# Four convolution and attention layers on eight images: the last two images' tail in a written order, and a normalised image transposed in its own tile

## The chip, the cores and the metric

The kernel runs on one core of a Trainium2 chip. A core has five engines with queues of their own: TensorE (PE, matrix products and transposes), VectorE (DVE), ScalarE (ACT), GpSimd (POOL) and SyncE (SP, which issues most transfers). Each works through its queue in order and waits for the others through semaphores. The metric is the device time of the whole program in microseconds (us). The profile is of one execution, with its own time, and shows every instruction on its engine.

## The reference

Eight images of 384 channels and 32 x 32 positions, all in fp32, go through four layers, each with a residual:

```python
x = x + L0(gn(x))   # attention over 8 heads, q, k, v by depthwise 3x3 + 1x1
x = x + L1(gn(x))   # four experts of two 384x384 layers, mixed by a router
x = x + L2(gn(x))   # quantised depthwise 3x3, then quantised 1x1
x = x + L3(gn(x))   # deformable attention
```

`gn` normalises over groups of channels; here there are 32 groups for 384 channels. In layer 3, q is a 1x1 product. A depthwise 5x5 convolution of stride 2 on q, with a batch norm and Gelu, gives for each of three groups of 128 channels and each of 256 places two offsets and a modulation. The normalised image is sampled bilinearly at the moved places (outside the image counts as zero), multiplied by the sigmoid of the modulation, and gives k and v. Six heads of 64 channels attend from 1024 queries to 256 keys; a 1x1 product with bias ends the layer.

## The kernel before

An image lies in SBUF as 128 partitions x 3 chunks (of 128 channels) x 1024 positions. `HALF` is 512 positions, which is one PSUM bank. `big` gives one of two PSUM tiles of two banks, `fbank` one of three single banks, `vbank` the one that is left. In SBUF, the pool `im` has five image-sized buffers that are used in turn, and there are tiles with fixed names (`hd0` to `hd3`, `h1`, `om0` to `om2`), which `third` and `pl.one` hand out.

Layer 0 runs over all images first, then routing. From there the kernel goes image by image: `layers(b)` is a generator that issues layers 2 and 3 of image b in steps and says with each `yield` about how long it leaves PE without work. `layer1(pl, b + 1)` is a list of units (matmuls of the expert layers: `ph`, L1491, and `y`, L1512) of the next image. The loop adds up the times and issues a unit whenever 2.6 us (`UNIT`) are due, so that the matmuls of the next image fill the gaps of this one. What comes out is a fixed order of instructions in each engine's queue; nothing is decided at run time.

Within `layers(b)`: the depthwise taps of layer 2 on DVE (L1634), the products `pw` (L1647), group norm (statistics on DVE; `gna` and `gnb`, L117 and L128, two tiny matmuls that sum over partitions; the reciprocal square root as a power on POOL, L98), the normalised image `h3`, q (`pq`, L1684), the transposes `px` of `h3` into positions x channels (L1707), written by ACT and DVE in turn into another image tile, `xT`; 25 taps of the offset convolution `off` on DVE (L1754), Gelu; `pom`, three products that spread offsets and modulation over all partitions (L1780, L1781), Tanh and positions on ACT and DVE; then for eight blocks of 128 image positions a bilinear weight `wt` (Abs and Relu on ACT, L1815 and L1818, product of x and y weights on POOL, L1819) and three matmuls that sum `xT` with it (`xsb`, `xs`, L1823); k and v (L1837, L1846). The attention has six units (three pairs of heads x two halves of the queries): scores `s` (L1862), exponentials `p` on ACT (L1879), the sum of the two key blocks' exponentials `p01` on POOL (L1924), `pav` (L1888), `pss` (L1901, the denominators), and on DVE the transposed copy `tu` (L1936) and the division. `pf` (L1991) is the last product, and DVE adds it to the image (L1999), which goes out.

For image 6 the loop stops at the step after Gelu (the `yield None`), issues the rest of image 7's layer 1, and then the tail begins: one step of image 7's layers for each step that image 6 has left, after that image 7 alone. Image 7 differs in a few ways: its layer-2 taps run during its layer 1, each as an output chunk is done (`convolve`); group norm of layer 2 is worked in afterwards (`layer2_last`: constants for the borders are added on DVE, then ACT normalises, L1605); its PSUM tiles are single banks (`pair`), and its h3 and xT lie in halves in the `hd` tiles.

Of the kernel before, what the change touches and what calls it, by code (L numbers as in the profile page):

```python
# [7 lines left out]
F32 = mybir.dt.float32  # L8
# [5 lines left out]
N = H * W  # L14
# [41 lines left out]
def tile_kernel(ctx: ExitStack, tc: tile.TileContext, i: dict, out: bass.AP):  # L56
# [1345 lines left out]
    def pair(last, name):  # L1402


        if last:
            return None, [fbank(f"{name}_{h}") for h in range(2)]
        t = big(name)
        return t, [t[:, :HALF], t[:, HALF:]]

# [154 lines left out]
    def convolve(pl, xt, c, h):  # L1564
# [7 lines left out]
        lo, hi = ((0, H // 2 - 1), (H // 2 - 1, H))[h]  # L1572
        nc.vector.tensor_scalar(
# [11 lines left out]
    def layer2_last(b, xt):  # L1585

        y = ahead["y"]
        ga, dm = gn_spread(gn_mean(ahead["st"], f"d2_{b}"), f"d2_{b}", fbank)
        edge = wd.tile([P, KC, 8], F32, name="edge_last")
        nc.vector.tensor_scalar(edge, edge2, ga[:, 0:1], None, ALU.mult)  # L1590
        for c in range(KC):
            dst = y[:, c, :].rearrange("p (h w) -> p h w", h=H)
            for d, e, axis in (
                (dst[:, 0 :: H - 1, :], edge[:, c, 0:2], 2), (dst[:, :, 0 :: W - 1], edge[:, c, 2:4], 1)
            ):
                nc.vector.tensor_tensor(d, d, e.unsqueeze(axis).to_broadcast(list(d.shape)), ALU.add)
            d = dst[:, 0 :: H - 1, 0 :: W - 1]
            nc.vector.tensor_tensor(
                d, d, edge[:, c, 4:8].rearrange("p (a b) -> p a b", a=2), ALU.add
            )  # L1600
        ss = gn_scale(ga, dm, f"d2_{b}", fbank)
        sums = wd.tile([P, KC], F32, name="sums_last")
        nc.vector.tensor_scalar(sums, sum2, ss[:, 1:2], None, ALU.mult)
        for c in range(KC):
            nc.scalar.activation(  # L1605
                y[:, c, :], y[:, c, :], AF.Identity, bias=sums[:, c : c + 1], scale=ss[:, 0:1]
            )
        yield 5.0
        yield from pointwise(b, xt, [y[:, c, :] for c in range(KC)])
# [29 lines left out]
    def pointwise(b, xt, y):  # L1639

        last = b == B - 1
        for m in range(KC):
            whole, pw = pair(last, f"pw{b}_{m}")
            for h in range(2):
                hs = slice(h * HALF, (h + 1) * HALF)
                for c in range(KC):
                    nc.tensor.matmul(  # L1647
                        pw[h], lhsT=upw2[:, c, m * P : (m + 1) * P], rhs=y[c][:, hs],
                        start=(c == 0), stop=(c == KC - 1),
                    )  # L1650
            xm = xt[:, m, :]
            outs = zip((xm[:, :HALF], xm[:, HALF:]), pw) if last else [(xm, whole)]
            for d, f in outs:
                nc.vector.scalar_tensor_tensor(d, f, mp, d, ALU.mult, ALU.add)
            nc.sync.dma_start(out=x2_dram[b, :, m, :], in_=xm)
            yield 0.0

    def layer3(pl, b, xt, put, general):

        last = b == B - 1  # L1660
# [4 lines left out]
        ss = gn_finish(st, f"d3_{b}", fbank if last else vbank)  # L1665
        yield 5.0

        if last:
            h3 = [third(pl, h, f"h3_{b}_{h}") for h in range(2)]
            for h in range(2):  # L1670
                for c in range(KC):
                    affine(h3[h][:, c, :], xt[:, c, h * HALF : (h + 1) * HALF], ss)
        else:
            t = pl.img(f"h3_{b}")
            for c in range(KC):
                affine(t[:, c, :], xt[:, c, :], ss)
            h3 = [t[:, :, :HALF], t[:, :, HALF:]]
        yield 3.0
        q = pl.img(f"q_{b}")
        for m in range(KC):  # L1680
            whole, pq = pair(last, f"pq3_{b}_{m}")
            for h in range(2):
                for c in range(KC):
                    nc.tensor.matmul(  # L1684
                        pq[h], lhsT=wq3[:, c, m * P : (m + 1) * P], rhs=h3[h][:, c, :],
                        start=(c == 0), stop=(c == KC - 1),
                    )
            if last:
                for h in range(2):
                    evac(q[:, m, h * HALF : (h + 1) * HALF], pq[h])  # L1690
            else:
                evac(q[:, m, :], whole)
            yield 0.0

        T2 = NT8 // 2
        if last:
            xT = [third(pl, 2 + h, f"xT_{b}_{h}").rearrange("p a n -> p (a n)") for h in range(2)]
        else:
            t = pl.img(f"xT_{b}").rearrange("p c n -> p (c n)")
            xT = [t[:, : T2 * C], t[:, T2 * C :]]  # L1700
        xT = [t.rearrange("p (t c) -> p t c", t=T2) for t in xT]
        for t in range(0, NT8, 2):
            h, t2 = divmod(t, T2)
            whole, px = pair(last, f"px_{b}_{t}")
            for k in range(2):
                for c in range(KC):
                    nc.tensor.transpose(  # L1707
                        px[k][:, c * P : (c + 1) * P],
                        h3[h][:, c, (t2 + k) * P : (t2 + k + 1) * P], ident,
                    )  # L1710
            if last:
                for k in range(2):
                    evac(
                        xT[h][:, t2 + k, :].rearrange("p (q c) -> p c q", c=KC),
                        px[k][:, :C].rearrange("p (c q) -> p c q", c=KC),
                    )
            else:
                evac(
                    xT[h][:, t2 : t2 + 2, :].rearrange("p t (q c) -> p t c q", c=KC),
                    whole.rearrange("p (t n) -> p t n", t=2)[:, :, :C].rearrange(  # L1720
                        "p t (c q) -> p t c q", c=KC
                    ),
                )
            yield 0.4

        if last:
            off = pl.one([P, KC, HALF], "h1", f"off_{b}").rearrange("p c n -> p (c n)")
            off = off[:, : NG * LS].rearrange("p (g h w) -> p g h w", g=NG, h=HS)
        else:
            off = pl.flat([P, NG, HS, HS], f"off_{b}")  # L1730
        src = q.rearrange("p g (h w) -> p g h w", h=H)

        def span(s):
            lo = max(0, (-s + 1) // 2)
            hi = min(HS - 1, (H - 1 - s) // 2)
            return lo, hi

        for t in (12, *range(12), *range(13, 25)):
            dy, dx = t // 5 - 2, t % 5 - 2
            (r0, r1), (c0, c1) = span(dy), span(dx)  # L1740

            gs = [None] if r1 - r0 + 1 == HS else range(NG)
            for g in gs:
                if g is None:
                    d = off.rearrange("p g h w -> p (g h) w")[:, :, c0 : c1 + 1]
                    f = q.rearrange("p g (h w) -> p (g h) w", h=H)[:, dy : : 2, :]
                else:
                    d = off[:, g, r0 : r1 + 1, c0 : c1 + 1]
                    f = src[:, g, 2 * r0 + dy : 2 * r1 + dy + 1 : 2, :]
                f = f[:, :, 2 * c0 + dx : 2 * c1 + dx + 1 : 2]  # L1750
# [484 lines left out]
```

## Time and profile before

| | us |
|---|---|
| median of three runs | 3484.91 (3483.53 to 3489.36) |
| profiled execution, its own time | 3480.29 |
| its span, first to last instruction | 3478.5 |
| PE busy in it | 3372.7 (97%) |
| DVE, ACT, POOL busy | 1708.2, 1298.5, 200.1 |
| last `y` of image 7's layer 1 ends | about 3266 |
| last `pf` ends | about 3471 |
| mean granted PE clock | 0.989 of full |

A group's busy time is the union of its instructions; "idle before" is the time its engine stood still ahead of it, and the releaser is the instruction whose semaphore came last. In fp32 each matmul leaves two records: one of 512 columns takes 0.86 us in a row of its kind and has two records of some 0.6 us that overlap. [...] Transfers play no part in what follows: the 16 DMA engines are busy for 18% of the time at most in any stretch of the tail.

### The profile page before, as it was taken

The page shows a single profiled execution, that of the slowest core. Times are in us where ns is not written, and L with a number is a line of the kernel's source. Part 1 is how long each engine was busy: PE and PEld are TensorE (multiplying, and loading weights), DVE is VectorE, ACT ScalarE, POOL GpSimd, SP SyncE. Part 2 cuts the span into 40 slices and gives each one's busy share as a digit, 9 for nine tenths or more (in the row PEclk, how much of TensorE's full clock was granted, in tenths as well). Part 3 has the DMA queues.
Part 4 walks back from the last instruction along what each step waited for, and adds up shares of the span by engine and source line. Part 5 has one row for each costly group of instructions (what it writes and reads, how often), then busy time and mean ns, then how long its engine had stood idle before and what let it go on. Part 6 is the DMA issues. An engine that isn't in the chain of part 4 may idle for free.

```text
span 3478.5 us, 44959 instructions
## 1 busy us (share of the span) xinstructions
PE 3372.7 (97%) x18599; PEld 1449.4 (42%) x18599; DVE 1708.2 (49%) x2926; ACT 1298.5 (37%) x1514; POOL 200.1 (6%) x231
## 2 busy tenths in 40 slices
PE   6999999999999999998999999999999999999888
PEld 2333434343434343443344445344453444434344
DVE  8942232323232323234266375663755637557763
ACT  5655444444444444433222322323223232331232
POOL 2100000000000000000000200102001010010022
PEclk9999999999999999999999999999999999999999
DMA  9972121212121212023600111101111011110000
GB/s 355 299 208 79 27 79 27 79 27 79 27 80 26 80 27 79 27 79 102 247 24 19 47 46 35 40 18 36 57 35 40 18 35 58 35 39 19 18 1 37
DMA packets 86260, 234.01 MB, mean 67 GB/s; under 512 B 21673, under 2 KB 21897, under 8 KB 79131
## 3 DMA queue, kind: packets, MB, share of 16 engines
q1 hardware_dynamic: 83882, 222.75, 19.8%
q10 hardware_dynamic: 1248, 4.72, 0.4%
q8 instruction: 150, 2.46, 0.3%
q0 software_dynamic: 912, 3.53, 0.3%
q14 instruction: 68, 0.55, 0.0%
HBM read 145.77 MB, written 75.59 MB: 64 GB/s over the span
## 4 chain that ended last, share of the span: by engine, by line
PE 43%; DVE 8%; DMA 1%; ACT 1%; POOL 0%; issue 0%; DVEq 0%; POOLq 0%; ACTq 0%; SPq 0%
PE y L1512 12%; PE ph L1491 10%; DVE y L1634 4%; PE pq L1684 4%; PE pw L1647 3%; PE pf L1991 3%; PE s L1862 2%; PE pav L1888 2%; DVE off L1754 1%; PE xsb L1823 1%; DVE hd L1477 1%; PE pss L1901 1%; PE pk L1837 1%; PE pv L1846 1%; PE plog L1231 1%; DMA o<-o 1%
## 5 line engine op out<-in xcount | busy, mean ns | idle before, releaser
L827 ACT ACTIVATE p<-s 128x1024 f32<-128x1024 f32 x512 | 496.3, 1021 | 365.7 <-PE s L820 365.5
L835 PE MATMUL pav<-p,vt 64*64 64x512 f32 x4096 | 494.5, 588 | 0.0
L1512 PE MATMUL y<-hd,w_sb 128*128 128x512 f32 x1080 | 487.1, 599 | 3.5 <-DVE hd L1477 3.5
L1491 PE MATMUL ph<-h,w_sb 128*128 128x512 f32 x1104 | 487.0, 595 | 1.9 <-ACT h L1440 1.8
L820 PE MATMUL s<-qk,qk 48*64 48x512 f32 x2944 | 355.0, 592 | 0.0
L1491 PEld LDWEIGHTS ph<-h,w_sb 128*128 128x128 f32 x1104 | 206.8, 190 | 262.3 <-issue 248.6
L1512 PEld LDWEIGHTS y<-hd,w_sb 128*128 128x128 f32 x1080 | 199.7, 191 | 249.0 <-issue 235.4
L835 PEld LDWEIGHTS pav<-p,vt 64*64 64x64 f32 x4096 | 167.4, 133 | 274.6 <-issue 274.4
L796 DVE COPY ta<-pav 128x512 f32<-128x512 f32 (+1 forms) x65 | 44.3, 682 | 475.3 <-PE pav L835 475.3
L1501 ACT ACTIVATE hd<-ph,b_sb 128x512 f32<-128x512 f32 x180 | 122.8, 682 | 309.9 <-PE ph L1491 309.9
L574 PE MATMUL pk<-xs,cws_sb 32*32 32x496 f32 (+3 forms) x3840 | 181.9, 605 | 38.8 <-POOL xs L402 29.4
L1754 DVE SCALAR_TENSOR_TENSOR off<-q,dw_sb,off 128x225 f32<-128x225 f32 (+3 forms) x432 | 215.8, 556 | 1.8
L1634 DVE SCALAR_TENSOR_TENSOR y<-h,tap,y 128x961 f32<-128x961 f32 (+1 forms) x168 | 203.0, 1229 | 0.5
L820 PEld LDWEIGHTS s<-qk,qk 48*64 48x64 f32 x2944 | 108.6, 133 | 212.0 <-issue 191.1
L1879 ACT ACTIVATE p<-s 128x1024 f32<-128x1024 f32 x96 | 96.2, 1023 | 165.7 <-PE s L1862 134.2
L81 DVE COPY qk<-pq 128x512 f32<-128x512 f32 x46 | 31.8, 692 | 251.8 <-PE pq L258 251.8
L1477 DVE TENSOR_TENSOR hd<-hd,cb 128x512 f32<-128x512 f32 x180 | 122.4, 685 | 37.7 <-ACT hd L1501 37.5
L574 PEld LDWEIGHTS pk<-xs,cws_sb 32*32 32x32 f32 (+1 forms) x3840 | 77.2, 111 | 141.9 <-issue 57.8
L1924 POOL TENSOR_TENSOR p<-p,p 128x1024 f32<-128x1024 f32 x48 | 113.4, 2364 | 330.0 <-ACT p L1879 329.9
L820 PE MATMUL s<-ql,ql 48*64 48x512 f32 x1024 | 128.2, 592 | 0.2 <-ACT p L827 0.2
L1991 PE MATMUL pf<-att,wp_sb 128*128 128x512 f32 x288 | 127.4, 597 | 0.0
L711 PE MATMUL pv<-wv_sb,g 128*128 128x384 f32 x384 | 127.1, 489 | 0.0
(341 smaller groups left out, 3734.5 us busy)
## 6 DMA issues: line engine op xcount, KB each, us to landing
rqk<-y SPq DMA_DIRECT2D x96, 256.0 KB
g<-rqk SPq DMA_DIRECT2D x96, 256.0 KB
xs<-in_xs_dram SPq DMA_DIRECT2D x56, 384.0 KB
g<-rv SPq DMA_DIRECT2D x48, 256.0 KB
xh<-in_x_dram SPq DMA_DIRECT2D x48, 256.0 KB
f<-in_x_dram SPq DMA_DIRECT2D x24, 512.0 KB
f<-o SPq DMA_DIRECT2D x24, 512.0 KB
o<-ot SPq DMA_DIRECT2D x42, 256.0 KB
```

Of the source, the lines that this page charges most:

```text
L574: nc.tensor.matmul(banks[r][cols[q]].rearrange("p (h w) -> p h w", w=W)[:, :, c0:c1], lhsT=cws[rs, c, 2 * h + g, x, w], rhs=src[rs, :, c0 ...
L711: nc.tensor.matmul(pv[:, :C], lhsT=acts[b][2][:, c, t * P : (t + 1) * P], rhs=w_in[2][:, c, :], start=(c == 0), stop=(c == KC - 1),)
L820: nc.tensor.matmul(s[64 * k : 64 * k + 64, j * HALF : (j + 1) * HALF], lhsT=kt[r, k0 : k0 + 64], rhs=qt[r, h * HALF : (h + 1) * HALF], sta ...
L827: nc.scalar.activation(p, s, AF.Exp, scale=scale)
L835: nc.tensor.matmul(pav[k][64 * j : 64 * j + 64, :], lhsT=vts[b % 2][r, kc, 2 * hd : 2 * hd + 2, :].rearrange("p a b -> p (a b)"), rhs=p[r, ...
L1477: nc.vector.tensor_tensor(hd, hd, state["cb"], ALU.mult)
L1491: nc.tensor.matmul(ph, lhsT=w1[:, e, c, dc * P : (dc + 1) * P], rhs=state["h1"][c], start=(c == 0), stop=(c == KC - 1),)
L1512: nc.tensor.matmul(y, lhsT=w2[:, e, dc, m * P : (m + 1) * P], rhs=state[h, k], start=(k == 0), stop=(k == NE * KC - 1),)
L1634: nc.vector.scalar_tensor_tensor(d, f, tap2[:, c, t : t + 1], d, ALU.mult, ALU.add)
L1684: nc.tensor.matmul(pq[h], lhsT=wq3[:, c, m * P : (m + 1) * P], rhs=h3[h][:, c, :], start=(c == 0), stop=(c == KC - 1),)
L1754: nc.vector.scalar_tensor_tensor(d, f, dw3[:, t : t + 1], d, ALU.mult, ALU.add)
L1991: nc.tensor.matmul(pf[:, hs], lhsT=wp3[:, pr, m * P : (m + 1) * P], rhs=att[:, pr, hs], start=(pr == 0), stop=(pr == NPAIR3 - 1),)
```

## The change

Four things are done.

1. For all images, h3 is laid out as 8 blocks of positions x 3 chunks x 128, and its transpose is written back into the same tile, block by block (`turned`, `rows_by_channel`). An image needs one image tile fewer, and q's matmuls read four runs of 128 positions.
2. Image 6 goes five steps further before the remaining layer-1 units of image 7: the rest of its transposes, `pom` and what follows it up to the first sampling weights. Its sampling matmuls then stand behind the last `y` and ahead of image 7's layer 2.
3. Image 7's layers 2 and 3 are written out as `last_image`, which calls `fill(n)` at set places to issue the next n steps of image 6. Group norm of layer 2 is begun ahead of the last chunk's taps (`last_norm`); the border constants of two chunks are added on POOL. The q product of group 0 is followed by this group's 25 taps, then q and transposes of the rest, then the taps of groups 1 and 2, between which image 6's attention is issued (after the 5th, 10th and 17th position 1, 2 and 2 steps). Image 6's last units and `pf` stand beside image 7's sampling and first units.
4. Image 6's k is copied by ACT, and the check of the denominators' range (`in_range`) is split: images 0 to 5 ahead of image 7's attention, 6 and 7 at the end.

Steps that only moved into functions of their own (`offsets`, `moved`, `sample`, `attend`) and image 7's old special cases in `layer3` are left out here.

```diff
+        if c == KC - 1 and h == 1:
+            ahead["norm"] = last_norm()
...
-    def layer2_last(b, xt):
-
-        y = ahead["y"]
-        ga, dm = gn_spread(gn_mean(ahead["st"], f"d2_{b}"), f"d2_{b}", fbank)
+    def last_norm():
+
+        name = f"d2_{B - 1}"
+        ga, dm = gn_spread(gn_mean(ahead["st"], name), name, fbank)
+        ss = gn_scale(ga, dm, name, fbank)
         edge = wd.tile([P, KC, 8], F32, name="edge_last")
-        nc.vector.tensor_scalar(edge, edge2, ga[:, 0:1], None, ALU.mult)
-        for c in range(KC):
-            dst = y[:, c, :].rearrange("p (h w) -> p h w", h=H)
-            for d, e, axis in (
-                (dst[:, 0 :: H - 1, :], edge[:, c, 0:2], 2), (dst[:, :, 0 :: W - 1], edge[:, c, 2:4], 1)
-            ):
-                nc.vector.tensor_tensor(d, d, e.unsqueeze(axis).to_broadcast(list(d.shape)), ALU.add)
-            d = dst[:, 0 :: H - 1, 0 :: W - 1]
-            nc.vector.tensor_tensor(
-                d, d, edge[:, c, 4:8].rearrange("p (a b) -> p a b", a=2), ALU.add
-            )
-        ss = gn_scale(ga, dm, f"d2_{b}", fbank)
         sums = wd.tile([P, KC], F32, name="sums_last")
+        nc.gpsimd.tensor_tensor(edge, edge2, ga[:, 0:1].unsqueeze(2).to_broadcast([P, KC, 8]), ALU.mult)
         nc.vector.tensor_scalar(sums, sum2, ss[:, 1:2], None, ALU.mult)
-        for c in range(KC):
-            nc.scalar.activation(
-                y[:, c, :], y[:, c, :], AF.Identity, bias=sums[:, c : c + 1], scale=ss[:, 0:1]
-            )
-        yield 5.0
-        yield from pointwise(b, xt, [y[:, c, :] for c in range(KC)])
+        for c in range(KC - 1):
+            border(nc.gpsimd, c, edge)
+        return ss, edge, sums
+
+    def border(engine, c, edge):
+
+        dst = ahead["y"][:, c, :].rearrange("p (h w) -> p h w", h=H)
+        for d, e, axis in (
+            (dst[:, 0 :: H - 1, :], edge[:, c, 0:2], 2), (dst[:, :, 0 :: W - 1], edge[:, c, 2:4], 1)
+        ):
+            engine.tensor_tensor(d, d, e.unsqueeze(axis).to_broadcast(list(d.shape)), ALU.add)
+        d = dst[:, 0 :: H - 1, 0 :: W - 1]
+        engine.tensor_tensor(d, d, edge[:, c, 4:8].rearrange("p (a b) -> p a b", a=2), ALU.add)
...
+        h3 = pl.img(f"h3_{b}").rearrange("p c n -> p (c n)").rearrange(
+            "p (t c n) -> p t c n", t=NT8, c=KC
+        )
+        for c in range(KC):
+            affine(h3[:, :, c, :], xt[:, c, :].rearrange("p (t n) -> p t n", t=NT8), ss)
...
+                        rhs=h3[:, h * NT8 // 2 : (h + 1) * NT8 // 2, c, :],
...
+        xT = h3.rearrange("p t c n -> p t (c n)")
...
+            evac(rows_by_channel(xT, t), turned(b, h3, t))
...
+    def turned(b, src, t):
+
+        px = big(f"px_{b}_{t}")
+        for k in range(2):
+            for c in range(KC):
+                nc.tensor.transpose(
+                    px[:, k * HALF + c * P :][:, :P], src[:, (t + k) % src.shape[1], c, :], ident
+                )
+        return px.rearrange("p (t n) -> p t n", t=2)[:, :, :C].rearrange(
+            "p t (c q) -> p t c q", c=KC
+        )
+
+    def rows_by_channel(xT, t):
+        return xT[:, t : t + 2, :].rearrange("p t (q c) -> p t c q", c=KC)
...
+    def sample(b, xT, om, accumulators, weights, result, fill=nothing):
...
-        xps = [xsb[:, :LS], xsb[:, HALF : HALF + LS], xs2[:, :LS]]
+        fill(2)
+        xps = accumulators()
...
             if t == 0:
                 yield 2.0
+                fill(2)
...
+        fill(4)
...
+    def attend(pl, b, xt, put, general, q, xs, fill=nothing):
...
+        copy = nc.scalar.copy if b == B - 2 else nc.vector.tensor_copy
+        copy(kt.rearrange("p m n -> p (m n)"), pk[:, : NPAIR3 * LS])
...
             ps, due3 = exps(0, scores(*units[0])), None
+            fill(1)
...
+                if u < KC:
+                    fill(1)
...
+    def in_range(units, k):
+
+        rec = rec3[:, units, :].rearrange("p u q -> p (u q)")
+        okt = pl.flat(list(rec.shape), f"okt3_{k}")
+        nc.vector.tensor_scalar(okt, rec, R_LO, None, ALU.is_ge)
+        nc.vector.scalar_tensor_tensor(okt, rec, R_HI, okt, ALU.is_le, ALU.mult)
+        nc.vector.tensor_reduce(oks[:, k : k + 1], okt, AX.X, ALU.min)
+
+    def last_image(pl, xt, fill):
+
+        b, y = B - 1, ahead["y"]
+        halves = [slice(h * HALF, (h + 1) * HALF) for h in range(2)]
+
+        def banks(name, m):
+            if m != 1:
+                return [fbank(f"{name}_{m}_{h}") for h in range(2)]
+            t = big(f"{name}_{m}")
+            return [t[:, hs] for hs in halves]
+
+        fill(8)
+        ss, edge, sums = ahead["norm"]
+        for c in range(KC):
+            if c == KC - 1:
+                border(nc.vector, c, edge)
+            for hs in halves if c == 0 else [slice(0, N)]:
+                nc.scalar.activation(
+                    y[:, c, hs], y[:, c, hs], AF.Identity, bias=sums[:, c : c + 1], scale=ss[:, 0:1]
+                )
+        fill(1)
+        st = small.tile([P, 2 * KC, 6], F32, tag="gn_st", name=f"st_d3_{b}")
+        for m in range(KC):
+            pw = banks("pw_last", m)
+            for c, h in [(c, h) for c in range(KC) for h in range(2)]:
+                nc.tensor.matmul(
+                    pw[h], lhsT=upw2[:, c, m * P : (m + 1) * P], rhs=y[:, c, halves[h]],
+                    start=(c == 0), stop=(c == KC - 1),
+                )
+            for h in range(2):
+                d = xt[:, m, halves[h]]
+                nc.vector.scalar_tensor_tensor(d, pw[h], mp, d, ALU.mult, ALU.add)
+                nc.vector.bn_stats(st[:, 2 * m + h, :], d)
+            nc.sync.dma_start(out=x2_dram[b, :, m, :], in_=xt[:, m, :])
+        fill(2)
+        name = f"d3_{b}"
+        ga, dm = gn_spread(gn_mean(st, name), name, fbank)
+        fill(1)
+        ss = gn_scale(ga, dm, name, fbank)
+        fill(1)
+        h3 = [third(pl, h, f"h3_{b}_{h}").rearrange("p a n -> p (a n)") for h in range(2)]
+        h3 = [t.rearrange("p (t c n) -> p t c n", c=KC, n=P) for t in h3]
...
+        def query(m):
+            pq = banks("pq_last", m)
+            for c, h in [(c, h) for c in range(KC) for h in range(2)]:
+                nc.tensor.matmul(
+                    pq[h], lhsT=wq3[:, c, m * P : (m + 1) * P], rhs=h3[h][:, :, c, :],
+                    start=(c == 0), stop=(c == KC - 1),
+                )
+            for h in range(2):
+                nc.scalar.copy(q[:, m, halves[h]], pq[h])
+
+        query(0)
+        for _ in offsets(off, q, [0]):
+            pass
+        query(1)
+        query(2)
+        xT = [t.rearrange("p t c n -> p t (c n)") for t in h3]
+        for t in range(0, NT8, 2):
+            h, t2 = divmod(t, NT8 // 2)
+            nc.scalar.copy(rows_by_channel(xT[h], t2), turned(b, h3[h], t))
+        fill(1)
+        steps = {4: 1, 9: 2, 16: 2}
+        for k, _ in enumerate(offsets(off, q, [1, 2])):
+            fill(steps.get(k, 0))
+        nc.scalar.activation(offf, offf, AF.Gelu, bias=bo3, scale=so3)
+        g2, wts = (third(pl, 2 + k, f"lo{k}_{b}").rearrange("p a n -> p (a n)") for k in range(2))
+        om = [g2[:, : NG * LS], g2[:, NG * LS :], offt[:, NG * LS :]]
...
+        def accumulators():
+            f = [fbank(f"xs_{b}_{k}") for k in range(2)]
+            return [f[0][:, :LS], f[0][:, LS:], f[1][:, :LS]]
...
+        xs = yield from sample(
+            b, Rows(), om, accumulators, weights,
+            lambda: om[1].rearrange("p (g s) -> p g s", g=NG), fill,
+        )
+        in_range(slice(0, (B - 2) * NU3), 0)
+        yield from attend(pl, b, xt, put_image(b), False, q, xs, fill)
...
+            if b == B - 2:
+                for _ in range(5):
+                    next(this)
...
-        following = layers(B - 1)
-        for _ in this:
-            next(following)
-        for _ in following:
+        def fill(n):
+            for _ in range(n):
+                next(this, None)
+
+        for _ in last_image(pl, xs_img.pop(B - 1), fill):
             pass
-        okt = pl.flat([P, B * NU3 * 16], "okt3")
```

## The prediction

> **What bounds the kernel now.** First the page's busy times and its slices: TensorE (PE) is busy for 97% of the span, so it is the bound unless some stretch says otherwise.
>
> ```profile
> span 3478.5 us, 44959 instructions
> PE 3372.7 (97%) x18599; PEld 1449.4 (42%) x18599; DVE 1708.2 (49%) x2926; ACT 1298.5 (37%) x1514; POOL 200.1 (6%) x231
> PE   6999999999999999998999999999999999999888
> ```
>
> Only the first slice and the last three are not full. The table by windows of the loop over images (us, then busy us and count of PE, weight loads, DVE, ACT, POOL, then clock, DMA share, GB/s):
>
> ```profile
> 2790.00:3000.00 210.00, 209.38 (x611) 93.94 (x610) 120.93 (x180) 58.33 (x78) 19.48 (x16) 1.00 0.10 37
> 3235.00:3266.00 31.00, 31.00 (x73) 13.46 (x71) 26.06 (x43) 3.00 (x3) 0.00 (x0) 1.00 0.00 1
> ```
>
> Up to 3266 us, where the last expert matmul (L1512) is done, PE has no gap: nothing done there for DVE, ACT or buffers can help. The same table of the tail:
>
> ```profile
> 3266.00:3278.00 12.00, 1.52 (x6) 1.21 (x6) 9.38 (x28) 1.91 (x2) 0.55 (x1) 0.70 0.00 0
> ...
> 3343.00:3384.00 41.00, 30.51 (x114) 9.51 (x115) 39.35 (x56) 15.57 (x15) 14.69 (x6) 0.88 0.00 0
> 3384.00:3399.00 15.00, 15.00 (x36) 6.65 (x35) 6.07 (x9) 0.00 (x0) 0.00 (x0) 1.00 0.18 72
> 3399.00:3424.00 25.00, 20.56 (x81) 17.09 (x80) 5.75 (x10) 9.65 (x22) 4.36 (x8) 0.73 0.05 21
> ```
>
> PE stands still and its granted clock falls to 0.70 and 0.73. What it waits for is in PE's waits from 3140 us on (total, times, longest):
>
> ```profile
> PE pav L1888 <- DVE tu L1936: 9.5, 3, 6.1
> PE pw L1647 <- ACT y_last L1605: 6.3, 1, 6.3
> PE xsb L1823 <- POOL wt L1819: 6.3, 2, 4.1
> PE gnb_d L128 <- DVE dm_d L122: 3.5, 2, 2.0
> PE gna_d L117 <- DVE mv_d L111: 2.2, 1, 2.2
> PE s L1862 <- ACT p L1879: 1.7, 2, 1.5
> PE px L1707 <- ACT xT L79: 1.3, 1, 1.3
> ```
>
> With two small ones these come to 31.6 us. The second loss is the clock. Cut finely, it is exactly 0.50 from 3270.75 for 10.24 us, 3304.88 for 6.83, 3352.67 for 6.83, 3369.73 for 3.41 and 3407.28 for 13.65: 41.0 us in which PE was busy 3.97 + 5.09 + 3.64 + 3.37 + 13.41 = 29.5 us. At full speed that work takes half, so 14.7 us are lost. Ceiling for any reordering of the tail: 31.6 + 14.7 = 46 us.
>
> [...] all five stretches are whole multiples of 3.41 us and follow a gap. [...] Six taps of image 7, beside two POOL adds of the exponentials (timelines of DVE and POOL):
>
> ```profile
> 3343.61 7.51 DVE L1754 SCALAR_TENSOR_TENSOR off<-q,dw_sb,off 128x240 f32<-128x240 f32 x6
> ```
> ```profile
> 3344.99 5.36 POOL L1924 TENSOR_TENSOR p<-p,p 128x1024 f32<-128x1024 f32 x2 [25.94 <-ACT p L1879]
> ```
>
> At the 460 ns that such a tap averages from 3309 to 3343 us, six take 2.8 us, not 7.5. [...] The trace has loads of 1283 ns around Gelu and exp[...].
>
> **The change, part by part.** The instructions per engine hardly change: PE 10541 matmuls in both programs, DVE 3659 to 3658, ACT 1705 to 1710, POOL 267 to 274, SP 1110 in the same order (so no transfer is moved past another). Until image 6's third pair of transposes, near 3213 us, each engine's order is the same too. So only waits, clock and the form of operands can move the time.
>
> 1. *h3 and its transpose in one tile, all images.* One image buffer less per image. Each evacuation overwrites only the two blocks that its own transposes have just read, so it waits for what it waited for before. The q matmuls read 4 runs of 128 instead of 512 in a row; no such row exists, but L258's pq reads runs of 32 at 592 ns a record beside 592 ns of today's pq and 598 of y. Cost taken: 0. Bounds: 0, or 144 matmuls x 0.86 us x 5% = 6 us.
>
> 2. *Image 6's transposes, pom and sampling.* 12 transposes and 6 pom matmuls (2.6 + 3.9 us) move ahead of the remaining layer-1 units; their waits (1.35 + 0.62) lie under full PE and go. The 24 sampling matmuls (24 x 0.2 = 4.8 us) come right after the last y and cover the gap before gna (2.20) and most of that before gnb (2.01); left about 0.4 for the last weight on POOL and 0.6 before gnb. Image 6's old sampling wait (2.15) goes.
>
> 3. *Before pw_last.* After gnb comes the rsqrt (pow) on POOL, now queued behind the edge multiply and six border adds moved from DVE. POOL's pow takes 0.55, its 144-element product 0.49, its 192-element one 0.59; I take 0.55 for each of the seven, 3.9 us, of which some 3.4 are left once gnb is done, then pow 0.55, two DVE operations 0.3, and half a chunk of y_last on ACT (1.23 / 2, say 0.69): 5.5 us with semaphores, against 6.27. Bounds for a small POOL operation: 0.2 (its slope from 192 to 144 elements leaves 0.2 at zero), which makes the gap 2.5 us less, and 1.2, which makes it 4.5 more.
>
> 4. *Image 7's GN, q, taps.* Image 6's k and v matmuls (3.87 + 3.9 us) stand in the GN gap, so gnb's 1.47 goes. About 0.8 appears at px_7, where ACT evacuates q and transposes in turn. Image 6's s wait for ACT stays (1.3 for 1.5).
>
> 5. *Image 6's attention between image 7's taps.* This is the place that gets no better. pav waits on DVE's tu, which is queued behind taps that POOL's 2.36 us adds hold up. A unit of attention keeps PE for about 4 us; between two fills DVE has 5 to 7 tap positions of two groups, about 0.9 us each, and one or two holds: waits of about 4.8 and 4.3, as against 9.5 in all before. Gelu with its table loads (1.28 + 1.03 + 1.28) stands before the next exponentials on ACT: another 2.1 + 0.6. Sum 11.8.
>
> 6. *Image 7's sampling and attention.* Image 6's units and projection stand in front, so the weights' wait of 4.12 shrinks to about 2.2 (the POOL weights stand behind one add, 2.36). New: image 6's x update on DVE holds a score bank three times, 0.57 each, 1.7. The split range check goes to DVE earlier, in cover; at the end 192 elements replace 768 ahead of pok, which waits for the last x update anyway: 0.
>
> Waits after: 1.0 + 5.5 + 0.8 + 1.3 + 11.8 + 2.2 + 1.7 = 24.3, saving 7.3.
>
> *The clock.* [...] The longest old stretch, 13.65 us over sampling at 48 and 64 columns, loses its cause. Three gaps, each followed by one or two windows of 3.41 us that are half or more full: loss 6 us (4 to 8) for 14.7, saving 8.7.
>
> Sum: 16 us. The profiled execution took 3480.29 (span 3478.5), which gives 3464.3; the median of the runs is 4.6 higher at 3484.91, so the forecast is 3469.
>
> **Rivals.** (a) *New waits eat it.* Item 5 decides: two more 2.36 us holds on taps, a table switch [...] met by PE in the open, [...] 3481, not to be told from before (0.2%, 7 us, is what a measurement of this kernel can tell). For: DVE is busy 39.35 of 41 us there already. Against: before, all of image 6's waiting on taps lay there as well.
> (b) *Nearly all is recovered.* If POOL's border adds take 0.2 us[...], waits fall to 19 and the clock loss to 2: 25 saved, 3460. Against: the old trace granted half clock after gaps of 4 to 6 us, and three remain.
> (c) *Slower by the strided q operand.* 144 q matmuls x 0.86 = 124 us lie on the saturated path. At 13% more per matmul the gain is eaten, at 18.5% the kernel is over 0.2% slower; at 25% it would take 31 - 16 = 15 us more, 3500. For: it touches every image and PE has no slack. Against: the 592 ns of L258's rows.
> (d) *The order doesn't take effect* because a wait ties the moved work to something late (weights of image 6 behind POOL, a buffer): then items 2 and 4 fall out and item 3's gap stays, 3483.
>
> **How the numbers follow.** Forecast 0.66, rival a 0.12, b 0.12, c 0.06, d 0.04. The forecast's own range is 3463 to 3476 (items 1 and 3 at their bounds, clock 4 to 8). To leave out no more than 2 in 10 the range is taken to 3459 to 3482: b and a lie inside. Faster by over 0.2% (below 3478): forecast, b and a small part of a, 0.82; same: most of a, and d, 0.12; slower: c, 0.06.
>
> **What would show it.** Right: the loop's windows unchanged with q records at 592 ns; xsb_6 directly behind y; the gnas without a wait; pw_last's wait about 5 us with POOL's pow as its last link; half-clock stretches of about 15 to 20 us in place of 41; pav waiting on DVE about 9 us. Wrong: q records above 620 ns (c), a tail in which DVE's taps are held longer and ACT loads tables more than three times (a), or a POOL border add over 1 us.

## The result, and the profile after

| | before | after |
|---|---|---|
| median of the runs, us | 3483.93 (6 runs, 3482.68 to 3489.36) | 3466.12 (6 runs, 3463.13 to 3469.55) |
| profiled execution, its span | 3480.29, 3478.5 | 3463.13, 3461.3 |
| image 6's q to the last matmul ("tail" below) | 273.7 | 256.3 |
| of it, PE waits | 31.6 | 15.2 |
| of it, at half clock (PE busy in it) | 41.0 (29.5) | 23.9 (19.9) |

The ratio is 0.9947, with a 95% interval of 0.9934 to 0.9960: 18 us faster, by the interval 14 to 23. Forecast were 3469, 3459 to 3482. The tail is measured in each trace from the first `pq` matmul of image 6 to `pok`; every kernel here has the same matmuls in the same order on PE up to there, so that it tells a few us apart where whole runs, which spread over 6 us, don't. It comes from one profiled execution of each kernel; two pairs of profiles whose tails are the same program agree within 0.4 us (273.7 and 273.3, 256.3 and 256.7).

The page after (busy times, PE's slices):

```profile
span 3461.3 us, 44963 instructions
PE 3366.8 (97%) x18599; PEld 1445.9 (42%) x18599; DVE 1705.9 (49%) x2925; ACT 1302.4 (38%) x1519; POOL 204.4 (6%) x238
PE   6999999999999999998999999999999999999989
```

One slice at the end is under nine tenths, where three were. The windows (columns as before: us, busy us and count of PE, weight loads, DVE, ACT, POOL, then clock, DMA share, GB/s):

```profile
2790.00:3000.00 210.00, 208.15 (x608) 93.49 (x607) 119.67 (x177) 58.34 (x78) 19.45 (x16) 1.00 0.11 37
3271.40:3281.45 10.05, 6.20 (x53) 5.88 (x52) 7.36 (x19) 2.91 (x8) 5.06 (x11) 0.90 0.00 0
...
3334.00:3348.00 14.00, 8.61 (x28) 2.50 (x26) 13.61 (x21) 4.81 (x5) 5.01 (x3) 0.76 0.00 0
3364.00:3379.00 15.00, 13.45 (x62) 9.57 (x62) 5.85 (x8) 3.94 (x10) 5.91 (x7) 0.66 0.00 1
3379.00:3454.00 75.00, 73.94 (x248) 29.23 (x245) 38.10 (x57) 13.82 (x14) 16.47 (x7) 1.00 0.09 36
```

From 3379 us on PE is all but full at full clock. What is left lies in three places: ahead of `pw_last`, in image 6's attention between the taps, and at image 7's sampling. PE's waits name them (us in total, times, longest):

```profile
PE pav L1886 <- DVE tu L1935: 5.4, 1, 5.4
PE pw_last L2041 <- ACT y_last L2033: 3.3, 1, 3.3
PE s L1860 <- ACT p L1877: 2.1, 2, 1.2
PE xs L1812 <- POOL lo L1807: 1.5, 1, 1.5
PE s L1860 <- DVE x L2000: 1.0, 3, 0.3
PE s L1860 <- ACT h L2085: 0.7, 1, 0.7
PE px L1726 <- ACT h L2085: 0.7, 1, 0.7
PE gnb_d L128 <- DVE dm_d L122: 0.5, 1, 0.5
```

And the clock is 0.50 in three stretches, each of which begins inside a wait of PE: the two largest, and that of 1.5 us at image 7's sampling (windows cut at the clock's steps):

```profile
3279.54:3286.37 6.83, 4.92 (x6) 2.19 (x7) 4.57 (x11) 3.89 (x4) 0.00 (x0) 0.50 0.02 4
3340.98:3347.81 6.83, 5.22 (x14) 1.51 (x15) 6.71 (x16) 3.11 (x3) 1.38 (x1) 0.50 0.00 0
3368.29:3378.53 10.24, 9.77 (x34) 6.67 (x36) 1.80 (x4) 1.02 (x1) 1.96 (x4) 0.50 0.01 2
```

Their starts lie 18 and 8 times 3.41 us apart. In the 3.41 us ahead of each start, PE did this:

```profile
3276.13:3279.54 3.41, 1.47 (x12) 1.26 (x11) 2.73 (x9) 0.00 (x0) 3.07 (x8) 1.00 0.00 0
3337.57:3340.98 3.41, 0.00 (x0) 0.00 (x0) 3.27 (x5) 0.00 (x0) 0.00 (x0) 1.00 0.00 0
3364.88:3368.29 3.41, 2.33 (x21) 2.19 (x20) 3.31 (x3) 2.03 (x7) 3.07 (x3) 1.00 0.00 0
```

Only in the second did PE stand still throughout. In the first it stood still for 1.94 us, in the third for 1.08, amid matmuls of 48 columns. In the kernel before, the window ahead of the stretch at 3304.88 us had 1.87 us without work, while another with 1.50, between matmuls of 512 columns, kept a clock of 1.00 in itself and in the next (3345.84 to 3349.25 us):

```profile
3301.47:3304.88 3.41, 1.54 (x8) 1.06 (x6) 2.24 (x8) 3.41 (x5) 0.04 (x1) 1.00 0.00 0
3342.43:3345.84 3.41, 1.91 (x10) 0.60 (x8) 3.38 (x9) 3.03 (x4) 0.85 (x1) 1.00 0.02 5
```

At a clock of 0.50 the records of `pw_last` start 853 ns apart, at 1.00 429 ns. So PE's 19.9 us of work in the three stretches would take about half at 1.00: 10.0 us lost by this estimate, where it was 14.7. So waits gave 16.4 us and the clock 4.7, together 21.1, but the tail is only 17.4 shorter. The 3.7 us between lie in PE's own work: with what ran at half clock counted half, it is 227.5 us of the tail before and 231.2 after. Counting for each matmul what it adds to PE's busy time, `s` takes 1.1 us more, `pss` 1.0, `pav` 0.8, the sampling 0.6 and `pf` 0.4; `pom` takes 0.3 less. These rows are cut into smaller pieces after the change (image 6's `pf` takes 3 x 5.42 = 16.3 us between image 7's units, image 7's own 15.7 in one go). That the cutting is the cause fits, but no run shows it.

### The profile page after: what moved, and what is told of

Same layout as the page of the kernel before. It is cut to its first block, busy times and chain, and to the rows that moved or that the text cites. A ratio compares the mean times of both kernels' runs of the same rounds, so it can differ in the third digit from the quotient of the medians.

```text
span 3461.3 us, 44963 instructions
## 1 busy us (share of the span) xinstructions
PE 3366.8 (97%) x18599; PEld 1445.9 (42%) x18599; DVE 1705.9 (49%) x2925; ACT 1302.4 (38%) x1519; POOL 204.4 (6%) x238
## 4 chain that ended last, share of the span: by engine, by line
PE 42%; DVE 7%; DMA 1%; ACT 1%; POOL 1%; issue 0%; DVEq 0%; ACTq 0%; POOLq 0%; SPq 0%
PE y L1504 12%; PE ph L1483 10%; DVE y L1625 4%; PE pq L1666 3%; PE pf L1992 3%; PE pw L1637 3%; PE s L1860 2%; PE pav L1886 2%; PE pk L1831 1%; DVE hd L1469 1%; DMA o<-o 1%; DVE off L1762 1%; PE pss L1899 1%; PE pv L1842 1%; PE xsb L1812 1%; PE pw_last L2041 1%
## 5 line engine op out<-in xcount | busy, mean ns | idle before, releaser
L1504 PEld LDWEIGHTS y<-hd,w_sb 128*128 128x128 f32 x1080 | 199.7, 191 | 248.3 <-issue 233.8
L835 PEld LDWEIGHTS pav<-p,vt 64*64 64x64 f32 x4096 | 168.6, 133 | 273.3 <-issue 273.1
L1762 DVE SCALAR_TENSOR_TENSOR off<-q,dw_sb,off 128x225 f32<-128x225 f32 (+4 forms) x441 | 215.3, 541 | 2.6
```

What stands on the lines that cost most here:

```text
L835: nc.tensor.matmul(pav[k][64 * j : 64 * j + 64, :], lhsT=vts[b % 2][r, kc, 2 * hd : 2 * hd + 2, :].rearrange("p a b -> p (a b)"), rhs=p[r, ...
L1504: nc.tensor.matmul(y, lhsT=w2[:, e, dc, m * P : (m + 1) * P], rhs=state[h, k], start=(k == 0), stop=(k == NE * KC - 1),)
L1762: nc.vector.scalar_tensor_tensor(d, f, dw3[:, t : t + 1], d, ALU.mult, ALU.add)
```

## The experiments

All times are medians; ratios are to runs of the kernel before on the same chip.

| kernel | tail | half clock | median | ratio, 95% |
|---|---|---|---|---|
| before, again | 273.3 | 41.0 | 3484.4 | 1.0001, 0.9992 to 1.0010 |
| before, one tile in images 0 to 6 | 266.3 | 37.6 | 3476.9 | 0.9980, 0.9972 to 0.9988 |
| before, one tile in image 6 | 266.6 | 34.1 | 3478.2 | 0.9977, 0.9969 to 0.9986 |
| after, image 6 not early | 259.6 | 23.9 | 3473.4 | 0.9966, 0.9955 to 0.9978 |
| after | 256.3 | 23.9 | 3466.1 | 0.9947, 0.9934 to 0.9960 |
| after, own xT in images 0 to 5 | 256.7 | 23.9 | 3465.4 | 0.9946, 0.9932 to 0.9959 |
| after, borders on DVE | 253.6 | 20.5 | 3466.3 | 0.9951, 0.9935 to 0.9966 |
| after, matmuls added in the sampling | 252.5 | 13.7 | 3463.9 | 0.9936, 0.9921 to 0.9951 |
| after, matmuls added at three places | 250.3 | 6.8 | 3462.2 | 0.9935, 0.9919 to 0.9952 |
| borders on DVE and added matmuls | 248.3 | 0 | 3458.4 | 0.9925, 0.9911 to 0.9938 |
| borders on DVE, tu earlier, two products of image 6 left out (not to be compared) | 247.2 | 20.5 | 3459.9 | 0.9928, 0.9912 to 0.9945 |
| after, no POOL sums in image 6 | 245.0 | 6.8 | 3457.7 | 0.9916, 0.9901 to 0.9931 |
| borders on DVE, sums on PE | 245.2 | 0 | 3457.3 | 0.9919, 0.9906 to 0.9933 |

**One tile alone.** The prediction had put the tile change at nothing. On the kernel before, for images 0 to 6:

```diff
-            t = pl.img(f"h3_{b}")          # [P, KC, N]
+            both = pl.img(f"h3_{b}")...    # as [P, 8, KC, 128]
-            t = pl.img(f"xT_{b}")...
+            t = both...                    # the same tile
```

> The kernel before with part 1 of the change alone: images 0 to 6 have h3 as blocks and its transpose written back into the same tile (six image tiles per image in place of seven); nothing else moves. Theory A (the tile count decides where and when the next image's tiles o land, so that DVE waits longer for them and PE for h1): the loop's waits of ph for h grow from 1.8 us to 4 or 5, DVE's waits for o from 2.7 to 5 or more, time +2 to +3 us, about 3486. Rival B (such landings differ from execution to execution, whatever the tiles): time as before within 1 us, 3483 to 3485. Rival C of the prediction (the q operand in four runs is slower): q records above 592 ns, +6 us or more.

None of the three foresaw it: 7.4 us came off the tail. In the kernel before, ACT's waits from 3205 to 3300 us have this row:

```profile
ACT xT L79 <- PE pw L1647: 15.4, 1, 15.4
```

The copy of image 6's transpose into `xT` waited for image 7's `pw`, the last reader of `y_last`: the seventh image tile had to take a buffer that image 7's convolved image still held. That is why the transposes of blocks 4 to 7 stood behind `pw` at 3296 us, with `pom`, position arithmetic and sampling behind them. With one tile, PE's timeline has all four pairs at their natural place:

```profile
3217.13 0.82 PE L1709 MATMUL px<-ident_sb,h 128*128 128x128 f32 x6
3217.79 1.02 PE L1491 MATMUL ph<-h,w_sb 128*128 128x512 f32 x2
3218.65 1.48 PE L1709 MATMUL px<-ident_sb,h 128*128 128x128 f32 x12
3219.96 1.02 PE L1491 MATMUL ph<-h,w_sb 128*128 128x512 f32 x2
3220.83 0.87 PE L1709 MATMUL px<-ident_sb,h 128*128 128x128 f32 x6
```

`pom` (4 us) then falls into the gap of `gna` and `gnb`, and the waits of `px`, `pom`, `gna` and of image 6's first sampling weight are gone. The q operand in four runs costs nothing: 592 ns a record in the kernel after, as before.

**Image 6 alone.** The same edit under `if b == B - 2`.

> The kernel before with one tile for h3 and its transpose in image 6 alone. Theory (in the kernel before, image 6's transpose waits for an image buffer that comes free only in the tail; with its own h3 tile it doesn't): as with the tile for all images, image 6's four pairs of transposes stand together near 3220 us, the stretch from image 6's q to the end of the last matmul is about 266 us in place of 273.7, time about 7 us below before, 3477. Rival (the gain comes from the loop's images): the stretch stays at 273 to 274 us and the time at 3484.

266.6 us: the whole gain of the tile change is image 6's, as the theory had it.

**The loop.** In the profile after, the first matmuls of layer 1, `ph`, wait 4.6 us in the loop for their input, and 1.8 before; that input waits for a transfer. DVE's waits from 1800 to 3235 us, before:

```profile
DVE x L1437 <- DMA o<-o: 2.7, 4, 1.0
```

and after:

```profile
DVE x L1429 <- DMA o<-o: 5.3, 6, 1.5
```

The tile count might have moved these landings. So images 0 to 5 got a tile of their own again:

```diff
         xT = h3.rearrange("p t c n -> p t (c n)")
+        if b < B - 2:
+            xT = pl.img(f"xT_{b}")...
```

> The changed kernel, but images 0 to 5 write the transpose into a tile of its own again (seven image tiles). The tail is untouched. Theory A: ph's waits for h fall from 4.6 to about 2 us, DVE's waits for o from 5.3 to about 2.7, time 2 to 3 us less than the changed kernel, about 3463. Rival B: 3466, the waits anywhere from 1.8 to 5.

The waits for o were 6.4 us with seven tiles, and the time was that of the changed kernel: theory A falls. The kernel before itself, once more:

> The kernel before once more, for the spread of a profile. Theory (the landing of the next image's tiles differs between executions): from the router to image 6's q it takes anything from 1562 to 1569 us, ph's waits for h come to 2 to 6 us, and the stretch from image 6's q to the last matmul is again 273 to 275 us. Rival (the block layout costs 4 us in the loop): again 1562 us with waits under 2.5 us.

```profile
DVE x L1437 <- DMA o<-o: 5.8, 5, 1.6
```

The landings differ from execution to execution: from the router to image 6's q, the first profile of the kernel before took 1562.3 us, this one 1565.3 and the changed kernel's 1566.1. The spans hide nothing by it, since the part ahead of the router went the other way (1635.3, 1632.6 and 1631.7 us): image 6's q starts at 3197.6, 3197.9 and 3197.8 us, and the 17.2 us between the two spans are the tail's.

**Image 6 early.** The five steps ahead of the remaining units were left out, and `fill(8)` made `fill(13)`.

> The changed kernel without the five early steps: image 6's last transposes, pom and sampling stand behind image 7's layer 1, all else as in the changed kernel. Theory (the early steps cover the group norm chain of image 7 and the clock): gna and gnb wait about 4 us for DVE, px, pom and the first sampling weights another 2 to 5, and one more stretch of half clock costs 2 to 3 us: 8 to 11 us more, about 3475. Rival (image 6's pieces only change places with other fill): at most 2 us more, 3466 to 3468.

The tail grew by 3.3 us, the median by 7. The direction is the theory's; the tail's size is neither's, and the places are not the theory's: `gna` and `gnb` wait 0.4 us in all. What waits is the sampling:

```profile
PE xs L1812 <- POOL wt L1807: 5.2, 4, 4.4
```

and one stretch at half clock of 13.65 us begins in it. The tail explains only 3.3 of the 7 us. Where the rest comes from isn't shown: the intervals of the two ratios overlap, and the profiled execution's loop, 3 us longer than the changed kernel's, differs as much between executions of one kernel.

**Borders.** `last_norm` with the edge product and `border` on `nc.vector`.

> The changed kernel with the edge product and the border constants of chunks 0 and 1 on DVE in place of POOL. Theory from the trace (POOL's seven operations end 0.3 us after the power could have begun, DVE would take about 1 us for what stands ahead of y_last): pw_last's wait grows from 3.35 us to about 4.2, time within 2 us of the changed kernel, about 3467. Rival from the prediction (POOL's queue is what bounds this gap): the wait falls by 1 us or more, to 2.3 or less.

My theory was wrong: the wait fell, as the rival taken from the prediction said, but by 0.85 us and not by 1 or more.

```profile
PE pw_last L2041 <- ACT y_last L2033: 2.5, 1, 2.5
```

In the changed kernel POOL works through its queue like this:

```profile
3276.34 0.70 POOL L1586 TENSOR_TENSOR edge_last<-edge,ga_d 128x24 f32<-128x24 f32 x1 [0.61 <-DVE ga_d L119]
3277.11 1.57 POOL L1598 TENSOR_TENSOR y_last<-y_last,edge_last 128x64 f32<-128x64 f32 x4
3278.64 0.36 POOL L1600 TENSOR_TENSOR y_last<-y_last,edge_last 128x4 f32<-128x4 f32 x2
3278.94 0.55 POOL L98 TENSOR_TENSOR ss_d<-ve_d,mhalf 128x1 f32<-128x1 f32 x1
```

The four border adds take 0.29, 0.29, 0.33 and 0.79 us, the last beside a tap, which takes 0.90 where others of its form take 0.76. From the end of `gnb` to the start of the power it takes 0.84 us in the changed kernel and 0.39 with the borders on DVE; from the end of the power to the first `y_last` 1.09 and 0.65, since a tap stands ahead of `sums_last` in DVE's queue in the one and a short border add in the other. So POOL's queue accounts for about half of what the wait lost, at most, and DVE's order for the other half. The wait before `gnb` (0.5 us) went too, and one window of half clock. The tail is 2.7 us shorter; the median, at 3466.3 of four runs, doesn't show it.

**The clock.** Matmuls that nothing reads were put where PE waits or works thinly: four of 384 columns ahead of `pw_last`, six ahead of image 6's second `pav`, one of 256 after each of six sampling blocks of image 7.

```diff
+        warm("warm_a", 4)                      # ahead of the loop over pw_last
+                if b == B - 2 and u == 1:
+                    warm("warm_b", 6, src=ps[1])
+            if b == B - 1 and t in (1, 2, 3, 4, 5, 6):
+                warm("", 1, spare3[0])         # in sample()
```

> The changed kernel with 16 added matmuls that nothing reads: four of 384 columns ahead of pw_last, six of 384 ahead of image 6's second pav, and one of 256 after each of six sampling blocks of image 7 (1.9 to 3.9 us of PE work at each place). Theory [...]: half clock falls from 23.9 us to 10 or less, the matmuls lie mostly in the waits, and the stretch from image 6's q to the last matmul shrinks from 256.3 to about 251, time 3461. Rival (thin stretches aren't what halves the clock): half clock stays above 20 us, and the time grows by 1 to 4 us, 3467 to 3470.

With more work the tail is 6 us shorter: half clock is down to 6.8 us, and the waits of `pw_last` and `xs` are gone from PE's list (`pom` has a new one of 2.7). With those in the sampling alone:

> The changed kernel with one matmul of 256 columns that nothing reads after each of six sampling blocks of image 7, and no others: 6 x 0.43 = 2.6 us of work, of which some 1.5 us lie in the wait for the POOL weights. Theory (PE working through matmuls of 48 and 64 columns counts as thin, and keeps the clock at half): the 10.24 us stretch near 3368 shrinks to 3.4 or goes, the other two stay, and the stretch from image 6's q to the last matmul is 252 to 254 us in place of 256.3. Rival (only waiting halves the clock): the stretch stays, and the work is added: 257 to 258.

```profile
3283.57:3290.40 6.83, 4.22 (x5) 1.83 (x6) 4.64 (x12) 3.89 (x4) 0.64 (x2) 0.50 0.01 4
3345.01:3351.84 6.83, 4.88 (x12) 1.48 (x13) 6.76 (x15) 2.77 (x3) 1.04 (x1) 0.50 0.00 0
```

The 10.24 us stretch is gone, the other two stand, and the tail is 3.8 us shorter. The added matmuls filled most of the wait (0.21 us are left of 1.55) and made the work less thin, and this run doesn't tell the two apart. In the next one the wait goes while the sampling is as thin as before (its 48 records in 5.56 us), and the clock is 1.00 there too: without the wait, this thin work ran at full clock.

**POOL's adds.** Why does `pav` wait 5.4 us? Image 6's `p01` was left out (denominators from the first key block only):

```diff
+                if b == B - 2:
+                    p01 = ps[0]
```

> The changed kernel without image 6's sums of the two key blocks' exponentials on POOL (six of 2.4 to 2.7 us): the denominators are taken from the first block alone, so image 6's output is not the reference's. Theory (the adds hold the taps, and tu stands behind them): the taps of 2.70 and 2.72 us fall to 0.7, pav's wait of 5.4 falls to about 1.5, and the stretch from image 6's q to the last matmul is 250 to 252 us. Rival (tu's place in DVE's queue is what counts, and the adds are in cover): the wait stays above 4 and the stretch above 254.

The tail lost 11.3 us, twice what I expected. DVE's taps up to the first `tu`, in the changed kernel:

```profile
3331.38 10.53 DVE L1762 SCALAR_TENSOR_TENSOR off<-q,dw_sb,off 128x225 f32<-128x225 f32 x9
3341.83 0.71 DVE L1935 STREAM_TRANSPOSE tu<-pav 128x512 f32<-128x512 f32 x1
```

beside POOL's two adds:

```profile
3332.31 5.21 POOL L1923 TENSOR_TENSOR p<-p,p 128x1024 f32<-128x1024 f32 x2 [27.55 <-ACT p L1877]
```

Nine taps, most of them of 0.7 us, take 10.5 us, because two of them last 2.70 and 2.72. Without the adds no tap takes more than 0.75 us, the longest wait for `tu` is 1.5 us, that for the sampling weights (also on POOL, behind such adds) is gone, and with them two of the three stretches at half clock. PE's waits in the tail fall from 15.2 to 11.2 us, and its work at half clock from 19.9 to 4.7: by this estimate 4.0 us of the 11.3 are waits and some 7.6 the clock.

**tu earlier.** The steps of image 6 are issued after the 5th, 10th and 17th tap position, but DVE's queue doesn't follow that order: in the trace the first `tu` stands behind the 19th. Here DVE's order was held to the written one, with borders on DVE and one step each after the 5th, 13th and 19th position. These are three steps in place of five, and nothing else issues the missing two: two of image 6's three `pf` products are left out, with their additions to the image.

```diff
-        steps = {4: 1, 9: 2, 16: 2}
+        steps = {4: 1, 12: 1, 18: 1}
```

> The changed kernel with the border constants on DVE, and with DVE's order in the taps of groups 1 and 2 as written: image 6's first two tu stand after the 13th and some 16th of the 25 positions (before: after the 20th and the 25th), steps at 5, 13 and 19. Theory (pav waits because tu stands behind taps): the wait of 5.4 us falls below 2, the half clock near 3341 goes, the stretch from image 6's q to the last matmul is 247 to 250 us (253.6 with the border on DVE alone). Rival (the taps then come later, and Gelu and image 7's sampling take the wait over): 253 to 256.

The trace has 48 `pf` records in the tail where the others have 72, 10.5 us of PE work less, so tail and time can't be compared. With this work the tail would be about 257.7 us (an estimate: 247.2 and 10.5), longer than the 253.6 of the borders alone. The waits ahead of the missing work can be read. `pav` waited 0.8 us in all, but the taps and so Gelu came later:

```profile
PE pom L1771 <- ACT off L2091: 9.8, 1, 9.8
```

PE's waits in the tail come to 19.7 us, against 13.8 with the borders alone. The theory was right about `pav` and no further: the wait moved and grew, as the rival had it.

**Better versions.** First the borders on DVE with the added matmuls (three at the first place):

> The changed kernel with the border constants on DVE and 15 matmuls that nothing reads at the three places: three ahead of pw_last, six ahead of image 6's second pav, six in image 7's sampling. Theory (the two gains stand apart): the stretch from image 6's q to the last matmul is 246 to 249 us, time about 3459. Rival (the warm clock leaves DVE as what bounds the same stretch, and the border operations delay it): as with the added matmuls alone, 250 us and 3462.

248.3 us and no half clock at all. Then, in place of useless matmuls, useful ones: image 6's first five denominators are summed over both key blocks on PE instead of on POOL.

```diff
-                p01 = pl.flat([P, N], f"p01_{b}_{u}")
-                nc.gpsimd.tensor_tensor(p01, ps[0], ps[1], ALU.add)
+                if b == B - 2 and u < 5:
+                    p01 = ps                   # sums() accumulates both in pss
+                else:
+                    p01 = [pl.flat([P, N], f"p01_{b}_{u}")]
+                    nc.gpsimd.tensor_tensor(p01[0], ps[0], ps[1], ALU.add)
```

> The changed kernel with the border constants on DVE, three matmuls that nothing reads ahead of pw_last, and image 6's denominators of its first five units summed over both key blocks on PE (two more matmuls of 512 columns a half, 0.86 us a unit, 4.3 us in all) in place of POOL's adds. Theory (the adds cost the tail 11 us by holding taps and weights; PE gives back 4.3 us or less, since part of it lies in waits): no tap above 1 us, one stretch of half clock at most, the stretch from image 6's q to the last matmul 243 to 246 us, time about 3455. Rival (the extra matmuls take the place of the waits, and the clock falls somewhere else): 248 us or more, as with the added matmuls, 3458 to 3459.

```profile
PE pav L1895 <- DVE tu L1949: 2.9, 2, 1.4
PE s L1869 <- ACT p L1886: 1.2, 1, 1.2
PE s L1869 <- DVE x L2014: 1.0, 3, 0.3
PE s L1869 <- ACT h L2100: 0.7, 1, 0.7
PE px L1735 <- ACT h L2100: 0.7, 1, 0.7
PE pw_last L2056 <- ACT y_last L2047: 0.5, 1, 0.5
```

These are all of PE's waits in the tail: 7 us, and no half clock. Nothing of the computation is left out in it, and by its median it is the fastest such version here, 3457.3 against 3483.6 (0.9919, 0.9906 to 0.9933), 9 us below the changed kernel. Whether it is faster than the version with added matmuls the intervals don't tell; the tails, 245.2 and 248.3, say so. The sums on PE were not run without the other two edits; with the borders on DVE alone the tail is 253.6.

## Why the prediction was right, and where it was not

The bound was read rightly in what mattered: there were 46 us to be had in the tail, some of it waits and some clock. (That PE has no gap up to 3266 us goes too far. The 19th slice is an 8 in both pages; around the routing PE waits 7.1 us for `gmean` and 6.9 for `plog`, which the change doesn't touch.) The time, 3466.1, is 3 us under the forecast. But the terms erred in both directions.

- *Item 1, the tile, taken as 0.* This step failed. "It waits for what it waited for before" looked at the reads and writes inside an image, and not at which buffer the removed tile had taken. Alone, on the kernel before, the tile gave 7.4 us, of 17.4 in all. The row of ACT's waits that shows it was in the profile before. The q operand, rival c, cost nothing, as argued.
- *Item 2.* Of the waits put down to the early steps, `px`, `pom` and image 6's first weight went with the tile already. What the early steps add is 3.3 us of tail.
- *Item 3.* 5.5 us forecast, 3.3 measured. Three of the four border adds of 64 elements take about 0.3 us and those of 4 elements 0.2, not 0.55, and some run while `gnb` is under way: the power starts 0.84 us after `gnb` and not 3.4. That POOL's queue bounds the gap was right in part. It is about half, at most, of the 0.85 us that the borders on DVE took off; the rest is DVE's part between the power and `y_last`, put at 0.3 us, which takes 1.09.
- *Item 4.* 0.8 and 1.3 forecast; 0.65, 0.69 and 1.2 measured.
- *Item 5.* 11.8 forecast, 6.3 measured (5.4 and one of 0.9 behind the table load of 1.28). Two taps beside POOL's adds did take 2.70 and 2.72 us, with `tu` behind them; the second wait for `tu` did not come.
- *Item 6.* 2.2 and 1.7 forecast, 1.55 and 1.0 measured.
- *The clock.* 6 us forecast, 10.0 measured. Three gaps were counted, ahead of `pw_last` (5.5 us forecast) and the two of item 5 (4.8 and 4.3). That shorter ones cost no clock was an assumption, and the traces don't bear it out: the stretches at 3304.88 and 3369.73 us, which the prediction lists, begin in gaps of 2.15 us (soon after one of 1.47) and 2.77, and in the changed kernel two begin in waits of 3.35 and 1.55 us. "The longest old stretch loses its cause" was wrong with it: the sampling, with the wait of 1.55 us inside it, still has 10.24 us at a clock of 0.50.

So waits were 9 us too dear, the clock 4 us too cheap, the tile's gain was booked under other items, and 3.7 us more of PE's own work were not foreseen; that the sum came within 3 us is luck in good part, because these cancel. Rival a did not come; what it rests on, taps that take longer beside POOL's adds (2.70 and 2.72 us, at most 0.75 without the adds), is nevertheless a large part of the 11.3 us that these adds still cost, only not more than before.

## What to carry to other kernels

When a change removes a tile, ask who had to give up the buffer it took: an evacuation that waits 15.4 us for another image's reader was the sign here, and without it the tail was 7.4 us shorter. In a tail where TensorE waits for several engines, price a GpSimd operation by what it holds up on VectorE and by the clock that goes with the waits, not by its own time. Here six adds of 2.4 to 2.7 us, with two taps of 2.70 and 2.72 beside them, came to 11.3 us of tail; with five of the sums on PE (`pss` takes 1.94 us a unit with them and 1.03 without), beside two other edits, the tail was 245.2 us, the shortest of those that leave nothing out. And look at the granted clock beside the waits, since a wait of 1.55 us amid matmuls of 48 and 64 columns went here with 10.24 us at a clock of 0.50.

## What the runs showed of the hardware that I had not expected

- Sixteen added matmuls made the kernel faster: half clock fell from 23.9 to 6.8 us, the tail by 6.0 us and the median from 3466.1 to 3462.2.
- A wait of 1.55 us inside a run of 48- and 64-column matmuls went with 10.24 us of half clock. The same 24 sampling products without that wait (5.56 us in one go, with the sums on PE) ran at a clock of 1.00. In the 3.41 us ahead of the stretch PE had stood still for only 1.08 us; in the kernel before, 1.50 us between 512-column matmuls left it at 1.00. What decides it the traces don't say.
- Waiting for the same transfers (the images' tiles `o`, 512 KB each) cost DVE 2.7 us in one execution of the kernel before and 5.8 in another, with the issues at the same places in the program.
